# Selective scan on one NeuronCore: two states per VectorE scan where the products with C are on VectorE, over two PSUM banks

## The chip, the cores and the metric

The kernel runs on one core of a Trainium2 chip. The metric is the device time of one execution in microseconds.

## The reference

The whole network is a vision state-space block (layer 0) followed by linear attention and a small quantized feed-forward (layer 1), on 8 images of 96 channels and 64 x 64 pixels. Nearly all of the time goes into the selective scan of layer 0. For each image, for 4 directions k, 192 inner channels d and 16 states n, over the 4096 positions l:

```
delta = softplus(dts + dt_bias)                 # one step size per (k, d, l)
dA    = exp(delta * A)                          # A < 0, one per (k, d, n)
h     = dA * h + (delta * u) * B[k, n, l]       # the recurrence over l
y     = sum over n of h * C[k, n, l]  +  D * u
```

The four directions are rows and columns of 8 x 8 windows, each forward and backward. The four y are added. Layer norms, convolutions, a gate and the two products of layer 1 surround this.

## The kernel before

**Tiles.** A direction of an image is cut into 8 chunks of T = 512 positions. One chunk of one direction is a *unit*: 8 images x 4 directions x 8 chunks = 256 units, worked one after the other. A unit has 192 x 16 sequences. 128 partitions hold 64 channels for two halves of the states, so there are 3 groups of channels (j) and, for each, 8 columns of states, in two groups (g) of G = 4. That makes six *tiles* of four states: `TILES` lists (g, j). A unit runs through 24 *slots*, one for each state of each tile: slot = 4n + m.

**A slot.** Four engines work on a state:

- POOL (`inputs`, L946) makes `hb`, the input (delta u) x B of a whole tile, 128 x 2048, in SBUF.
- ScalarE (`decays`, L1062) makes `da` = exp(delta x A), 128 x 512, in a PSUM bank, for the slot two ahead. `da` has three banks.
- VectorE (L1123) scans: it runs the recurrence with `tensor_tensor_scan`, starting from the column of `carry` that holds the state's last value in the chunk before. Backward directions use reversed views.
- The product with C comes in two ways. For the first `u.banked[n]` states of tile n the scan writes back into the PSUM bank, and VectorE multiplies by C into `hb` (L1125). For the others the scan writes into `hb`, and POOL multiplies later (`outputs`, L952). `BANKED` gives the numbers by tile: 4, 0, 4, 0, 4, 2 in most units, and 4, 0, 4, 0, 4, 1 in the first eight units of each image but the first.

The last value of each state goes to `carry` by a ScalarE copy: one per state of the first kind, out of PSUM (L1126), one per tile for the rest, out of `hb` (L1131). The copy is put on `kept` and issued at the start of the next slot, in front of that slot's decay.

**The sums.** TensorE adds the products over the states into two PSUM banks, tagged y01 and y2 (`sums`, L972), adds the skip part D x u, or the y of a pass before, fetched by `before`, with an identity or diagonal matrix (L981), and ScalarE takes the result out (`gather`, L989 and L992).

**Step sizes.** `step_sizes` is a chain of six steps: a TensorE product into a bank of its own (tag dt, L911), Abs, Exp and Ln on ScalarE (L919, L921, L923), one VectorE step (L925), and the product with u on POOL (L928). Kind "a" is done once per unit (128 channels), kind "b" once per two units (64 channels of each). `spread` then copies delta and delta u to both halves of the partitions by DMA (L940). `fetched_dt`, `fetched_u` and `fetched_pair` load the chain's inputs (L886, L893, L899), `states` loads B and C, repeated over 64 partitions (L880).

**Order.** Each engine's instructions run in the order in which the program issues them. `plan` lists by hand what is issued in each slot after the scan, for this unit, the one before (`last`), the next (`nxt`) and the one after (`third`). After each slot, `advance` lets two side streams go on: the back end of the image before and the front end of the next one. SP issues all DMAs. [...] three for da, one for dt, f0 and f1 for the side streams, y01 and y2 for the sums.

Of the kernel before, what the change touches and what calls it, by code (L numbers as in the profile page):

```python
# [9 lines left out]
F32 = mybir.dt.float32  # L10
# [3 lines left out]
ALU = mybir.AluOpType  # L14
# [16 lines left out]
SPREAD = 5  # L31
HB = 6

BANKED = ((4, 0, 4, 0, 4, 1), (4, 0, 4, 0, 4, 2))

HOLD = 3
LAND = 11
# [6 lines left out]
def kernel(ctx: ExitStack, tc: tile.TileContext, a, out):  # L44
# [13 lines left out]
    dram = ctx.enter_context(tc.tile_pool(name="scratch", bufs=2, space=DRAM))  # L58
    psum = ctx.enter_context(tc.tile_pool(name="psum", bufs=1, space=PSUM))

    BANKS = {"da": 3, "dt": 1, "f0": 1, "f1": 1, "y01": 1, "y2": 1}

    def bank(tag, name):
        return psum.tile([P, T], F32, tag=tag, name=name, bufs=BANKS[tag])
# [9 lines left out]

    eps = const([P, 1], 1e-5, "eps")
    one = const([P, 1], 1.0, "one")
    ones_c = const([C, C], 1.0 / C, "ones_c")

    def centering(n, m, diagonal, name):
# [766 lines left out]
    for b in range(out.shape[0]):  # L846
        s = {"b": b, "done": set(), "live": b + 1 == out.shape[0]}
        images.append(s)
        for pair in (1, 0):
            for back in range(2):  # L850
                for i in range(NC):
                    u = Unit()
                    u.s, u.pair, u.back, u.k = s, pair, back, pair + 2 * back
                    u.c, u.start = (NC - 1 - i if back else i), i == 0
                    u.new, u.i = (pair, back, i) == (1, 0, 0), len(units)
                    u.bc, u.hb, u.delta, u.du = {}, {}, {}, {}
                    u.banked = BANKED[int(b == 0 or u.i % 32 >= NC)]
                    units.append(u)

    TILES = [(g, j) for g in range(2) for j in range(3)]  # L860
# [40 lines left out]
    def step_sizes(us, i):  # L901

        u, which = us[0], "ab"[len(us) - 1]
        if i == 0:
            u.ps = bank("dt", "dt")
            if which == "a":
                todo = [(u.ps, slice(0, P), u)]
            else:
                todo = [(u.ps[64 * h : 64 * h + 64], slice(P, DI), w) for h, w in enumerate(us)]
            for ps, d, w in todo:  # L910
                nc.tensor.matmul(ps, dt_w[32 * w.k : 32 * w.k + R + 1, d], w.dts, start=True, stop=True)  # L911
            u.nat = sp.tile([P, T], F32, tag="nat" + which, name="nat", bufs=1)
            if which == "a":
                u.nata = u.nat
            else:
                for w in us:
                    w.natb = u.nat
        elif i == 1:
            nc.scalar.activation(u.nat, u.ps, AF.Abs)  # L919
        elif i == 2:  # L920
            nc.scalar.activation(u.nat, u.nat, AF.Exp, scale=-1.0)  # L921
        elif i == 3:
            nc.scalar.activation(u.nat, u.nat, AF.Ln, bias=one)  # L923
        elif i == 4:
            nc.vector.scalar_tensor_tensor(u.nat, u.ps, 0.0, u.nat, ALU.max, ALU.add)  # L925
        else:
            x = u.ua if which == "a" else u.ub
            nc.gpsimd.tensor_tensor(x, u.nat, x, ALU.mult)  # L928
# [19 lines left out]
    def outputs(u, n):  # L948

        lo = u.banked[n]  # L950
        hb = u.hb[n][:, lo:, :]
        nc.gpsimd.tensor_tensor(hb, hb, u.bc[1, TILES[n][0]][:, lo:, :], ALU.mult)  # L952

    def before(u):

        src = u.s["u"][1] if u.k == 1 else u.s["y"][u.pair]
        u.plain = []
        for i, rows in enumerate((slice(0, P), slice(P, src.shape[0]))):
            t = sp.tile([P, T], F32, tag=f"u{i}", name=f"u{i}", bufs=1)[: rows.stop - rows.start]
            u.plain.append(into(t, src[rows, bass.ts(u.c, T)]))  # L960

    def sums(u, ns, m):

# [7 lines left out]
        for ps, n, i in todo:  # L971
            nc.tensor.matmul(  # L972
                ps, halves, u.hb[n][:, i, :], start=TILES[n][0] == 0 and m == 0, stop=False, skip_group_check=True
            )
        if ns[-1] == 5 and m == 1:
            first = u.k == 1
            for ps, w, x in (
                (u.p[0], dd_a if first else ident, u.plain[0]),
                (u.p[1][low] if first else u.p[1], dd_b if first else ident, u.plain[1]),
            ):  # L980
                nc.tensor.matmul(ps, w, x, start=False, stop=True, skip_group_check=True)  # L981

    def gather(u, i):

# [12 lines left out]
    def plan(u, last, nxt, third):  # L997

        at = [[] for _ in range(24)]

        def put(slot, f, *args):
            at[slot].append((f, args))

        if last:
            put(0, outputs, last, 5)
            put(0, before, last)
            for m in range(2):
                put(m, sums, last, (3, 4), 2 + m)
            for m in range(2):
                put(5 + m, sums, last, (5,), m)  # L1010
            put(7, states, u, 1, 1)
            put(10, gather, last, 0)
            put(11, gather, last, 1)
        for n in range(6):
            to = (u, n + 2) if n < 4 else (nxt, n - 4)
            if to[0]:
                put(4 * n + 1, inputs, *to)
        if third and u.i % 2:
            put(16, step_sizes, (nxt, third), 5)
        put(8, outputs, u, 1)  # L1020
        put(16, outputs, u, 3)
        for m in range(4):
            put(13 + m, sums, u, (0, 1), m)
            if m < 2:
                put(18 + m, sums, u, (2,), m)
                put(22 + m, sums, u, (3, 4), m)
        if nxt:
            for i, slot in enumerate((0, 2, 4)):
                put(slot, step_sizes, (nxt,), i + 3)
            put(4, spread, nxt, 0, (0, 1))  # L1030
            put(6, spread, nxt, 1, (0, 1))
            put(10, states, nxt, 0, 0)
            put(15, states, nxt, 1, 0)
            put(20, states, nxt, 0, 1)
            if u.i % 2 == 0:
                put(15, spread, nxt, 0, (2,))
                put(16, spread, nxt, 1, (2,))
        if third:
            put(1, fetched_dt, third)
            put(9, fetched_u, third)  # L1040
            for i, slot in enumerate((20, 22, 23)):
                put(slot, step_sizes, (third,), i)
            if u.i % 2:
                for i, slot in enumerate((9, 11, 12, 13, 15)):
                    put(slot, step_sizes, (nxt, third), i)
                put(17, spread, nxt, 0, (2,))
                put(18, spread, nxt, 1, (2,))
            elif u.i + 3 < len(units):
                put(21, fetched_pair, third, units[u.i + 3])
        return at  # L1050

    def at_index(i):
        return units[i] if 0 <= i < len(units) else None

    def decays(q):

        if q >= 24 * len(units):
            return
        u, (n, m) = units[q // 24], divmod(q % 24, G)
        g, j = TILES[n]  # L1060
        da[q] = bank("da", "da")
        nc.scalar.activation(  # L1062
            da[q], u.delta[j], AF.Exp, scale=a_neg[:, u.k, j, g * G + m : g * G + m + 1]
        )

    da, kept, side, carry = {}, [], [], None
    for u in units[:2]:
        fetched_dt(u)
    fetched_u(units[0])
# [6 lines left out]
    for what in range(2):  # L1076
        spread(units[0], what, range(3))
    fetched_u(units[1])
    for i in range(3):
        step_sizes(units[1:2], i)  # L1080
    inputs(units[0], 0)
    inputs(units[0], 1)
    decays(0)
    decays(1)

    def advance(n):

# [4 lines left out]
    for u in units:  # L1092
        last, nxt, third = (at_index(u.i + d) for d in (-1, 1, 2))
        if u.new:
# [7 lines left out]
            else:  # L1102
                final = back_end(b, u.s)
                last_kit = back_kit(None, "f0", True, kit_f)
                side.append(Stream(final[0][0](last_kit, range(1, NC)[::-1])))
        if third and third.new:
            drained(*side[-1:])
            all_issued()
        if u.start:
            carry = sp.tile([P, 24], F32, tag="carry", name="carry")  # L1110
        todo = plan(u, last, nxt, third)
        for slot in range(24):
            n, m = divmod(slot, G)
            g, j = TILES[n]
            q, hb, first_at = 24 * u.i + slot, u.hb[n], 0 if u.back else T - 1
            col = carry[:, 8 * j + g * G + m : 8 * j + g * G + m + 1]
            while kept:
                kept.pop(0)()
            decays(q + 2)
            d = da.pop(q)  # L1120
            banked = m < u.banked[n]
            dd, x = (d[:, ::-1], hb[:, m, ::-1]) if u.back else (d, hb[:, m, :])
            nc.vector.tensor_tensor_scan(dd if banked else x, dd, x, 0.0 if u.start else col, ALU.mult, ALU.add)  # L1123
            if banked:
                nc.vector.tensor_tensor(hb[:, m, :], d, u.bc[1, g][:, m, :], ALU.mult)  # L1125
                kept.append(lambda col=col, d=d, at=first_at: nc.scalar.copy(col, d[:, at : at + 1]))  # L1126
            elif m == G - 1:
                lo = 8 * j + g * G
                kept.append(
                    lambda c=carry[:, lo + u.banked[n] : lo + G].unsqueeze(2), h=hb[:, u.banked[n] :, :], at=first_at:  # L1130
                    nc.scalar.copy(c, h[:, :, at : at + 1])  # L1131
                )
            for f, args in todo[slot]:
                f(*args)
            place[0] = slot
# [2 lines left out]
    for f in kept:  # L1138
        f()
    outputs(u, 5)  # L1140
    before(u)
    for m in range(2):
        sums(u, (3, 4), 2 + m)
    for m in range(2):
        sums(u, (5,), m)
    gather(u, 0)
    gather(u, 1)
    all_issued()
# [76 lines left out]
```

## Time and profile before

| | |
|---|---|
| runs before (3) | 11338.22 / 11342.24 / 11354.75 us, median 11342.24 |
| the profiled execution | 11372.37 us, span of its instructions 11370.7 us |
| the scan phase | from 352 to 11092 us |
| granted TensorE clock | 0.822 |
| DMA engines, mean busy share in the scan phase | 0.85 |

The profile is one execution. Part 1 of the page has each engine's busy time, part 5 the groups of instructions by line with their count, mean duration and the idle time just before them with what ended it. The chain of waits lists which engine and line waited for which, the total in us, how often, and the longest. A line of the timeline has start and duration in us, engine, line, operation, what is written and read.

### The profile page before, as it was taken

How to read it: one execution, taken by the hardware profiler on the slowest of the kernel's cores; microseconds unless marked ns; L12 is line 12 of the kernel's file. 1: busy time of each engine (PE TensorE's matmuls, PEld its weight loads, DVE VectorE, ACT ScalarE, POOL GpSimd, SP SyncE). 2: the span in 40 equal slices, each digit the busy share in tenths (PEclk: the TensorE clock that was granted, in tenths of full speed). 3: DMA queues.
4: the chain of work that ended last, by engine and by line, in shares of the span. 5: the costliest groups of instructions: out<-in, count | busy, mean ns of one | idle time of the engine just before them, and what ended most of it. 6: DMA issues, size and time to landing. Idle time of an engine off the chain costs nothing. (4 is left out here: it accounts for less than half of the span.)

```text
span 11370.7 us, 97041 instructions
## 1 busy us (share of the span) xinstructions
PE 8567.3 (75%) x23270; PEld 2328.5 (20%) x23270; DVE 10367.4 (91%) x10828; ACT 7508.4 (66%) x14939; POOL 10398.7 (91%) x2783
## 2 busy tenths in 40 slices
PE   6577657887778877888678876788768887676677
PEld 2111112222122211222112221222212221111122
DVE  0799999999999999999999999999999999999991
ACT  3566656767666676667766676666766667666674
POOL 0799999999999999999999999999999999999990
PEclk8678778888788877889778887888878888787787
DMA  2788878898888888888888888889888888888872
GB/s 71 171 197 197 201 189 210 209 225 196 203 210 212 219 198 202 210 215 215 195 207 210 216 214 194 210 205 228 202 200 211 212 220 195 198 198 195 201 188 78
DMA packets 1081039, 2253.24 MB, mean 198 GB/s; under 512 B 419609, under 2 KB 420314, under 8 KB 949395
## 3 DMA queue, kind: packets, MB, share of 16 engines
q1 hardware_dynamic: 1080467, 2247.05, 81.3%
q8 instruction: 184, 3.01, 0.1%
q14 instruction: 388, 3.18, 0.1%
HBM read 1507.14 MB, written 336.69 MB: 162 GB/s over the span
## 5 line engine op out<-in xcount | busy, mean ns | idle before, releaser
L946 POOL TENSOR_TENSOR hb<-b,du 128x2048 f32<-128x2048 f32 x1536 | 6939.0, 4535 | 21.3 <-DMA du<-ua 14.3
L1062 ACT ACTIVATE da<-delta,w_a_logs 128x512 f32<-128x512 f32 x6144 | 4216.7, 689 | 696.3 <-DVE hb L1123 575.8
L972 PE MATMUL p<-hb,halves 128*64 128x512 f32 x12288 | 3822.7, 731 | 800.1 <-POOL hb L952 382.1
L1123 DVE TENSOR_TENSOR_SCAN da<-da,carry,hb 128x512 f32<-128x512 f32 x3087 | 3949.0, 1279 | 58.0 <-ACT da L1062 54.3
L952 POOL TENSOR_TENSOR hb<-hb,c 128x2048 f32<-128x2048 f32 (+2 forms) x768 | 2984.9, 3887 | 304.7 <-ACT carry L1131 252.2
L1123 DVE TENSOR_TENSOR_SCAN hb<-da,carry,hb 128x512 f32<-128x512 f32 x2289 | 2781.0, 1264 | 57.7 <-ACT da L1062 56.7
L1125 DVE TENSOR_TENSOR hb<-da,c 128x512 f32<-128x512 f32 x3528 | 2440.5, 692 | 154.0 <-DVE da L1123 0.9
L1126 ACT COPY carry<-da 128x1 f32<-128x1 f32 x3528 | 554.9, 157 | 2351.6 <-DVE hb L1125 2341.1
L972 PEld LDWEIGHTS p<-hb,halves 128*64 128x64 f32 x12288 | 916.2, 161 | 3540.7 <-issue 2129.5
L434 PE MATMUL conv<-f0im,taps 97*128 97x512 f32 (+1 forms) x2088 | 903.5, 664 | 95.9 <-ACT f0pre L490 54.3
L928 POOL TENSOR_TENSOR ua<-nat,ua 128x512 f32<-128x512 f32 x256 | 327.3, 1279 | 257.5 <-DMA b<-xd 257.5
L1123 DVE TENSOR_TENSOR_SCAN da<-da,hb 128x512 f32<-128x512 f32 x441 | 537.7, 1219 | 26.0 <-POOL hb L946 24.6
L925 DVE SCALAR_TENSOR_TENSOR nat<-dt,nat 128x512 f32<-128x512 f32 x384 | 259.5, 676 | 238.9 <-ACT nat L923 238.9
L911 PE MATMUL dt<-dts,dt_w 7*64 7x512 f32 (+1 forms) x1024 | 450.0, 657 | 16.9 <-DVE nat L925 12.4
L981 PE MATMUL p<-u,ident 128*128 128x512 f32 x768 | 438.3, 699 | 3.6 <-DMA u<-y 3.6
L376 PE MATMUL ctr<-f1b,cen_c 96*96 96x512 f32 x460 | 271.9, 697 | 193.4 <-DVE f1b L769 158.8
L434 PEld LDWEIGHTS conv<-f0im,taps 97*128 97x128 f32 (+1 forms) x2088 | 254.6, 174 | 681.6 <-issue 523.5
L1123 DVE TENSOR_TENSOR_SCAN hb<-da,hb 128x512 f32<-128x512 f32 x327 | 377.9, 1204 | 4.9 <-ACT da L1062 4.9
L382 PE MATMUL var<-f1b,ones_c 96*96 96x512 f32 x346 | 207.4, 684 | 153.6 <-ACT f1b L379 145.3
L792 POOL TENSOR_TENSOR f1b<-f1b,f1o 96x512 f32<-96x512 f32 x58 | 67.7, 1167 | 252.0 <-ACT f1o L790 251.9
L1131 ACT COPY carry<-hb 128x4 f32<-128x4 f32 (+2 forms) x768 | 146.8, 191 | 197.4 <-DVE hb L1123 184.8
L655 PE MATMUL cab<-f1m,cab_w 96*96 96x512 f32 x348 | 206.0, 719 | 90.9 <-ACT f1b L664 41.4
(416 smaller groups left out, 7710.5 us busy)
## 6 DMA issues: line engine op xcount, KB each, us to landing
b<-xd SPq DMA_DIRECT2D x1024, 512.0 KB
c<-xd SPq DMA_DIRECT2D x1024, 512.0 KB
delta<-nat SPq DMA_DIRECT2D x1536, 128.0 KB
du<-ua SPq DMA_DIRECT2D x1024, 128.0 KB
y<-yt SPq DMA_DIRECT2D x512, 256.0 KB
u<-y SPq DMA_DIRECT2D x384, 256.0 KB
ua<-u SPq DMA_DIRECT2D x256, 256.0 KB
du<-ub SPq DMA_DIRECT2D x512, 128.0 KB
```

Source lines behind the costliest of these rows:

```text
L376: nc.tensor.matmul(ps, cen_c, src, start=i == 0, stop=i == len(srcs) - 1)
L434: nc.tensor.matmul(ps, taps[:, t, lo : lo + n], im[:, r0 + dy : r0 + dy + 8, dx : dx + HW], start=t == 0, stop=t == 8,)
L911: nc.tensor.matmul(ps, dt_w[32 * w.k : 32 * w.k + R + 1, d], w.dts, start=True, stop=True)
L928: nc.gpsimd.tensor_tensor(x, u.nat, x, ALU.mult)
L946: nc.gpsimd.tensor_tensor(hb, u.bc[0, g], u.du[j].unsqueeze(1).to_broadcast([P, G, T]), ALU.mult)
L952: nc.gpsimd.tensor_tensor(hb, hb, u.bc[1, TILES[n][0]][:, lo:, :], ALU.mult)
L972: nc.tensor.matmul(ps, halves, u.hb[n][:, i, :], start=TILES[n][0] == 0 and m == 0, stop=False, skip_group_check=True)
L981: nc.tensor.matmul(ps, w, x, start=False, stop=True, skip_group_check=True)
L1062: nc.scalar.activation(da[q], u.delta[j], AF.Exp, scale=a_neg[:, u.k, j, g * G + m : g * G + m + 1])
L1123: nc.vector.tensor_tensor_scan(dd if banked else x, dd, x, 0.0 if u.start else col, ALU.mult, ALU.add)
L1125: nc.vector.tensor_tensor(hb[:, m, :], d, u.bc[1, g][:, m, :], ALU.mult)
L1126: kept.append(lambda col=col, d=d, at=first_at: nc.scalar.copy(col, d[:, at : at + 1]))
```

## The change

In units whose product counts allow it, states with products on VectorE are taken in pairs. `da` becomes two tiles of two banks each. A scan of 1024 elements runs over both banks of a pair, and one product of 1024 elements follows. So that the second state of the pair does not go on from the first's last value, the element at the border gets its decay set to zero, and the carry it would have had is put in by ScalarE beforehand: the input at that element becomes input + decay x carry (an Identity activation of one element), and then zero is copied over the decay. In the first unit of a pass there is no carry, and only the zero is written. One ScalarE copy then takes both last values to `carry`. States with products on POOL are scanned singly as before, out of one half of a pair tile.

The counts become 4, 0, 4, 0, 4, 2 in the first eight units of each image but the first, and in the other units 4, 0, 4, 0, 4, 2 and 4, 0, 4, 0, 4, 4 in turn.

With four banks for da the dt bank is gone: the chain of kind "a" writes into the y01 bank and that of kind "b" into y2, between a gather and the next sums. For that, `plan` moves the gathers from slots 10 and 11 to 4 and 8, the first sums from slots 13 to 16 to slots 15 and 16, those of tile 2 one slot later, and the step sizes to slots 6 to 20 of the unit before their use (kind "b" one slot later than now). The addition of the skip part becomes a function of its own (`added`, slots 2 and 6), its fetch is made in the unit itself (slots 18 and 21) and not at slot 0 of the next; `spread` for the first two groups moves from slots 4 and 6 to 2 and 3, `fetched_u` from 9 to 5, `fetched_dt` to slot 14 of the unit before. At the end of an image the front stream is drained one unit earlier.

```diff
-BANKED = ((4, 0, 4, 0, 4, 1), (4, 0, 4, 0, 4, 2))
+BANKED = (((4, 0, 4, 0, 4, 2),), ((4, 0, 4, 0, 4, 2), (4, 0, 4, 0, 4, 4)))
...
-    BANKS = {"da": 3, "dt": 1, "f0": 1, "f1": 1, "y01": 1, "y2": 1}
+    BANKS = {"f0": 1, "f1": 1, "y01": 1, "y2": 1}
...
-                    u.banked = BANKED[int(b == 0 or u.i % 32 >= NC)]
+                    some = BANKED[int(b == 0 or u.i % 32 >= NC)]
+                    u.banked = some[u.i % len(some)]
...
-            u.ps = bank("dt", "dt")
+            u.ps = bank({"a": "y01", "b": "y2"}[which], "dt")
...
         lo = u.banked[n]
+        if lo == G:
+            return
...
+            put(2, added, last, 0)
+            put(4, gather, last, 0)
...
+            put(6, added, last, 1)
+            put(8, gather, last, 1)
             put(7, states, u, 1, 1)
-            put(10, gather, last, 0)
-            put(11, gather, last, 1)
+        if nxt:
+            put(2, spread, nxt, 0, (0, 1))
+            put(3, spread, nxt, 1, (0, 1))
+        if third:
+
+            put(5, fetched_u, third)
+            for i, slot in enumerate((6, 8, 9, 10, 12, 20)):
+                put(slot, step_sizes, (third,), i)
+            if u.i % 2:
+                for i, slot in enumerate((10, 12, 13, 14, 16, 17)):
+                    put(slot, step_sizes, (nxt, third), i)
...
-            put(13 + m, sums, u, (0, 1), m)
+        for m, slot in enumerate((15, 15, 16, 16)):
+            put(slot, sums, u, (0, 1), m)
             if m < 2:
-                put(18 + m, sums, u, (2,), m)
+                put(19 + m, sums, u, (2,), m)
                 put(22 + m, sums, u, (3, 4), m)
+        put(18, before, u, 0)
+        put(21, before, u, 1)
...
+        fourth = at_index(u.i + 3)
+        if fourth:
+            put(14, fetched_dt, fourth)
+            if u.i % 2 == 0:
+                put(21, fetched_pair, third, fourth)
...
-        da[q] = bank("da", "da")
+        if m % 2 == 0:
+            da[q // 2] = psum.tile([P, 2, T], F32, tag="da", name="da", bufs=2)
+        d = da[q // 2]
         nc.scalar.activation(
-            da[q], u.delta[j], AF.Exp, scale=a_neg[:, u.k, j, g * G + m : g * G + m + 1]
+            d[:, m % 2, :], u.delta[j], AF.Exp, scale=a_neg[:, u.k, j, g * G + m : g * G + m + 1]
         )
+        if m % 2 and m < u.banked[n]:
+
+
+            i, at = (0, T - 1) if u.back else (1, 0)
+            edge, col = d[:, i, at : at + 1], column(j, g, m - 1 + i)
+            if not u.start:
+                x = u.hb[n][:, m - 1 + i, at : at + 1]
+                nc.scalar.activation(x, edge, AF.Identity, bias=x, scale=carry[0][:, col : col + 1])
+            nc.scalar.copy(edge, zero)
...
+    def scanned_state(u, slot):
+
+        n, m = divmod(slot, G)
+        g, j = TILES[n]
+        q, hb = 24 * u.i + slot, u.hb[n]
+        end = slice(0, 1) if u.back else slice(T - 1, T)
+        while kept:
+            kept.pop(0)()
+        decays(q + 2)
+        banked = m < u.banked[n]
+        if banked and m % 2:
+            return
+        pair = da[q // 2] if m % 2 == 0 else da.pop(q // 2)
+        if banked:
+            col = column(j, g, m + u.back)
+            d, x = (t.rearrange("p m l -> p (m l)") for t in (pair, hb[:, m : m + 2, :]))
+        else:
+            col = column(j, g, m)
+            d, x = pair[:, m % 2, :], hb[:, m, :]
+        if u.back:
+            d, x = d[:, ::-1], x[:, ::-1]
+        init = 0.0 if u.start else carry[0][:, col : col + 1]
+        nc.vector.tensor_tensor_scan(d if banked else x, d, x, init, ALU.mult, ALU.add)
+        if banked:
+            nc.vector.tensor_tensor(hb[:, m : m + 2, :], pair, u.bc[1, g][:, m : m + 2, :], ALU.mult)
+            del da[q // 2]
+            ends, lo, hi = pair, m, m + 2
+        elif m == G - 1:
+            ends, lo, hi = hb[:, u.banked[n] :, :], u.banked[n], G
+        else:
+            return
+        to = carry[0][:, column(j, g, lo) : column(j, g, hi)].unsqueeze(2)
+        kept.append(lambda: nc.scalar.copy(to, ends[:, :, end]))
...
-        if third and third.new:
+        if u.i + 3 < len(units) and units[u.i + 3].new:
             drained(*side[-1:])
             all_issued()
```

More of the change, by code (lines that the diff above doesn't have):

```diff
@@ L76 @@
     one = const([P, 1], 1.0, "one")
+    zero = const([P, 1], 0.0, "zero")
     ones_c = const([C, C], 1.0 / C, "ones_c")
@@ L855 @@
                     u.new, u.i = (pair, back, i) == (1, 0, 0), len(units)
-                    u.bc, u.hb, u.delta, u.du = {}, {}, {}, {}
-                    u.banked = BANKED[int(b == 0 or u.i % 32 >= NC)]
+                    u.bc, u.hb, u.delta, u.du, u.plain = {}, {}, {}, {}, {}
+                    some = BANKED[int(b == 0 or u.i % 32 >= NC)]
+                    u.banked = some[u.i % len(some)]
                     units.append(u)
@@ L950, in outputs, with before, added @@
         lo = u.banked[n]
+        if lo == G:
+            return
         hb = u.hb[n][:, lo:, :]
         nc.gpsimd.tensor_tensor(hb, hb, u.bc[1, TILES[n][0]][:, lo:, :], ALU.mult)
-    def before(u):
+    def before(u, i):
         src = u.s["u"][1] if u.k == 1 else u.s["y"][u.pair]
[L957 to L960, printed above, removed]
+        rows = (slice(0, P), slice(P, src.shape[0]))[i]
+        t = sp.tile([P, T], F32, tag=f"u{i}", name=f"u{i}", bufs=1)[: rows.stop - rows.start]
+        u.plain[i] = into(t, src[rows, bass.ts(u.c, T)])
+    def added(u, i):
+        ps, first = u.p[i], u.k == 1
+        w = ((dd_a, dd_b)[i]) if first else ident
+        nc.tensor.matmul(
+            ps[0:64] if first and i else ps, w, u.plain[i], start=False, stop=True, skip_group_check=True
+        )
     def sums(u, ns, m):
@@ L974, in sums @@
             )
[L975 to L981, printed above, removed]
     def gather(u, i):
@@ L1005, in plan @@
             put(0, outputs, last, 5)
-            put(0, before, last)
             for m in range(2):
                 put(m, sums, last, (3, 4), 2 + m)
+            put(2, added, last, 0)
+            put(4, gather, last, 0)
             for m in range(2):
                 put(5 + m, sums, last, (5,), m)
+            put(6, added, last, 1)
+            put(8, gather, last, 1)
             put(7, states, u, 1, 1)
-            put(10, gather, last, 0)
-            put(11, gather, last, 1)
+        if nxt:
[8 more added lines that the diff above has]
+                    put(slot, step_sizes, (nxt, third), i)
         for n in range(6):
@@ L1017, in plan @@
                 put(4 * n + 1, inputs, *to)
-        if third and u.i % 2:
-            put(16, step_sizes, (nxt, third), 5)
         put(8, outputs, u, 1)
         put(16, outputs, u, 3)
-        for m in range(4):
-            put(13 + m, sums, u, (0, 1), m)
+        for m, slot in enumerate((15, 15, 16, 16)):
+            put(slot, sums, u, (0, 1), m)
             if m < 2:
-                put(18 + m, sums, u, (2,), m)
+                put(19 + m, sums, u, (2,), m)
                 put(22 + m, sums, u, (3, 4), m)
+        put(18, before, u, 0)
+        put(21, before, u, 1)
         if nxt:
[L1028 to L1031, printed above, removed]
             put(10, states, nxt, 0, 0)
@@ L1037, in plan @@
                 put(16, spread, nxt, 1, (2,))
[L1038 to L1045, printed above, removed]
-                put(17, spread, nxt, 0, (2,))
-                put(18, spread, nxt, 1, (2,))
-            elif u.i + 3 < len(units):
-                put(21, fetched_pair, third, units[u.i + 3])
+            else:
+                put(17, spread, nxt, 0, (2,))
+                put(19, spread, nxt, 1, (2,))
+        fourth = at_index(u.i + 3)
[3 more added lines that the diff above has]
+                put(21, fetched_pair, third, fourth)
         return at
@@ L1053, in at_index, with column @@
         return units[i] if 0 <= i < len(units) else None
+    def column(j, g, m):
+        return 8 * j + g * G + m
     def decays(q):
@@ L1060, in decays @@
         g, j = TILES[n]
-        da[q] = bank("da", "da")
+        if m % 2 == 0:
+            da[q // 2] = psum.tile([P, 2, T], F32, tag="da", name="da", bufs=2)
+        d = da[q // 2]
         nc.scalar.activation(
-            da[q], u.delta[j], AF.Exp, scale=a_neg[:, u.k, j, g * G + m : g * G + m + 1]
+            d[:, m % 2, :], u.delta[j], AF.Exp, scale=a_neg[:, u.k, j, g * G + m : g * G + m + 1]
         )
-    da, kept, side, carry = {}, [], [], None
+        if m % 2 and m < u.banked[n]:
[5 more added lines that the diff above has]
+            nc.scalar.copy(edge, zero)
+    da, kept, side, carry = {}, [], [], [None]
     for u in units[:2]:
@@ L1078 @@
     fetched_u(units[1])
-    for i in range(3):
-        step_sizes(units[1:2], i)
     inputs(units[0], 0)
@@ L1084 @@
     decays(1)
+    for i in range(6):
+        step_sizes(units[1:2], i)
+    fetched_dt(units[2])
+    def scanned_state(u, slot):
[26 more added lines that the diff above has]
+            ends, lo, hi = hb[:, u.banked[n] :, :], u.banked[n], G
+        else:
+            return
+        to = carry[0][:, column(j, g, lo) : column(j, g, hi)].unsqueeze(2)
+        kept.append(lambda: nc.scalar.copy(to, ends[:, :, end]))
     def advance(n):
@@ L1109 @@
         if u.start:
-            carry = sp.tile([P, 24], F32, tag="carry", name="carry")
+            carry[0] = sp.tile([P, 24], F32, tag="carry", name="carry")
         todo = plan(u, last, nxt, third)
         for slot in range(24):
[L1113 to L1132, printed above, removed]
+            scanned_state(u, slot)
             for f, args in todo[slot]:
@@ L1140 @@
     outputs(u, 5)
-    before(u)
     for m in range(2):
@@ L1145 @@
         sums(u, (5,), m)
+    for i in range(2):
+        added(u, i)
     gather(u, 0)
```

## The prediction

> **What bounds the kernel now.** I read the page's part 1 first, then the busy times over the scan phase (first to last scan, 352 to 11092 us), then the groups, then the chain of waits, then the timeline.
>
> ```profile
> PE 8567.3 (75%) x23270; PEld 2328.5 (20%) x23270; DVE 10367.4 (91%) x10828; ACT 7508.4 (66%) x14939; POOL 10398.7 (91%) x2783
> ```
>
> ```profile
> 352.00:11092.00 10740.00, 8145.56 (x22246) 2185.72 (x22245) 10313.25 (x10697) 7281.15 (x14607) 10371.12 (x2747) 0.82 0.85 205
> ```
>
> The second line has PE, PEld, DVE, ACT, POOL in that order. In the 10740 us of scans VectorE is busy 10313 (96%) and POOL 10371 (97%): the two share the bound, and nothing before or after that phase changes here. The groups say what VectorE does and how little it waits:
>
> ```profile
> L1123 DVE TENSOR_TENSOR_SCAN da<-da,carry,hb 128x512 f32<-128x512 f32 x3087 | 3949.0, 1279 | 58.0 <-ACT da L1062 54.3
> L1123 DVE TENSOR_TENSOR_SCAN hb<-da,carry,hb 128x512 f32<-128x512 f32 x2289 | 2781.0, 1264 | 57.7 <-ACT da L1062 56.7
> L1125 DVE TENSOR_TENSOR hb<-da,c 128x512 f32<-128x512 f32 x3528 | 2440.5, 692 | 154.0 <-DVE da L1123 0.9
> ```
>
> VectorE waits about 115 us in all for decays, because ScalarE runs two states ahead: in the trace the median decay ends 2.3 us before its scan. That lead is what the change spends. The decisive row is in the chain of waits:
>
> ```profile
> ACT carry L1126 <- DVE hb L1125: 2341.1, 2311, 4.1
> ```
>
> The carry copy reads what the scan (L1123) wrote, yet it waits for the product (L1125). The timeline, VectorE first and then ScalarE in the same three microseconds:
>
> ```profile
> 5518.47 1.28 DVE L1123 TENSOR_TENSOR_SCAN da<-da,carry,hb 128x512 f32<-128x512 f32 x1
> 5519.79 0.69 DVE L1125 TENSOR_TENSOR hb<-da,c 128x512 f32<-128x512 f32 x1
> 5520.40 1.28 DVE L1123 TENSOR_TENSOR_SCAN da<-da,carry,hb 128x512 f32<-128x512 f32 x1
> ```
>
> ```profile
> 5520.51 0.16 ACT L1126 COPY carry<-da 128x1 f32<-128x1 f32 x1 [1.04 <-DVE hb L1125]
> 5520.71 0.69 ACT L1062 ACTIVATE da<-delta,w_a_logs 128x512 f32<-128x512 f32 x1
> ```
>
> The scan ends at 5519.75, the product at 5520.48, the copy starts at 5520.51, and the decay queued behind it follows. Over all 3528 pairs in the trace no copy starts earlier than 33 ns after the product's end; those that waited started 33 to 35 ns after it.
>
> [...] The changed copy and product also read the same two banks. [...]
>
> **The change, part by part.**
>
> *Counts.* States with products on VectorE: before 56 units x 13 + 200 x 14 = 3528. After: 56 x 14 + 100 x 14 + 100 x 16 = 3784, in 1892 pairs. The other states fall from 2616 to 2360.
>
> *VectorE's own work.* I use start-to-start times in the trace: a single scan 1.175 us; scan to product 1.316; product to next scan 0.608; so 1.924 per state with a product. A product of 1024 elements: L227, a tensor_tensor of 1728 elements, took 1957 ns against 692 for 512, a slope of 1.04 ns, so +0.533. The scan has no second size in the trace. If its fixed part is that of the product (0.075) plus what the carry operand adds (1279 - 1219 = 0.06), 1.040 us remain for 512 elements; I take +1.06. A pair then takes 1.316 + 1.06 + 0.608 + 0.533 = 3.52 us, against 2 x 1.924 = 3.85. Saved: 1892 x 0.33 = **-624**. Bounds: -0.22 per pair (scan saves nothing) to -0.40: -420 to -760. The 256 states that come over cost 256 x (1.924 - 1.175) = **+192**.
>
> *POOL* loses those 256 products at 2984.9 / 2616 = 1.14 us: -292. That would matter only if POOL remained the bound.
>
> *The new wait.* Decays are issued two states ahead. With pairs, slot m of a pair issues the next pair's first decay, and slot m+1 first issues this pair's carry copy, then the next pair's second decay, then (new) the edge: an Identity of one element with two pointer operands that adds decay x carry to the input, and a copy of zero into the decay. ScalarE takes them in that order, and the next scan needs all of them. So where a pair follows a pair, from the product's end: 0.033 to the copy, 0.19 copy to decay (median spacing), 0.689 decay, 0.03 for the dependent next (L369 to L370: 675 ns apart, 642 long), 0.33 the fix (0.157 for a one-element copy, plus two operands at about 0.09), 0.03, 0.157 the zero, 0.033 to the scan: 1.49 us. Without a wait the scan would have started 0.084 before the product's end. The stall is **1.58 us**; in the first unit of each pass (1 in 8), which has no fix, 1.22. Mean 1.535. Bounds 1.33 (the two small ones overlap) to 1.75 (each takes 0.1 more).
>
> How often: the order of tiles is 4, 0, 4, 0, 4, then 2 or 4 states. Pair follows pair inside tiles 0, 2, 4 and from tile 4 to 5: 4 times. With 4 in tile 5 also inside it and on into the next unit: 6. So 156 x 4 + 100 x 6 = 1224 times x 1.535 = **+1879** (1628 to 2140). Queued behind the waiting copy on ScalarE are that decay, the edge and whatever side work follows; POOL and PE are not held by it. Where a single follows a pair, its decay came in the even slot: no stall.
>
> *What fills the stall.* Other VectorE work in those slots (643 side instructions in the trace; by its slots about 35% fall there, plus the 128 step-size steps moved to slot 16): 353 x 0.6 = **-212** (0 to -300).
>
> *Pair after singles*, 668 times: ScalarE has two single scans, 2.35 us, for two decays and the edge, 1.93, so 0.42 us are left for side work. By slot that averages 0.2 to 0.6 us and comes in lumps: I put 0.15 us each, **+100** (0 to 250).
>
> *Waits that go*: the 115 us for decays are counted anew above: **-120**.
>
> *Moved and free.* Step sizes run in slots 6 to 20 of the unit before instead of 20 to 4; counts are equal. POOL's step product (1.28 us) now stands between two input products, which in the trace end a median 5.8 us before their scan. SP's fetch of ua comes two slots after the transfer that reads it instead of three; SP waits 74.5 us for that now, and the next loads behind it have 14 slots (25 us) to their use. The skip inputs (u) are fetched some five slots earlier, dt thirteen. The step sizes take the sums' banks, so their matmul waits for the gathers (slots 4 and 8, before 10 and 11) and the next sums for the step. In PE's order the last sums and the skip need about 11 us between slots 22 and 4; six slots give 10.6 us today, 12 in the slower kernel. I take **0**, bounds 0 and +250. The fetch of the image after is drained one unit earlier: 0.
>
> *Sum*: -624 + 192 + 1879 - 212 + 100 - 120 = **+1215**. The profiled execution took 11372.37 (span 11370.7), 30 above the median of 11342.24; I add the difference to the median: 12557, rounded to **12,560 us**.
>
> **Rivals.**
>
> *The copy leaves when the scan ends* (would be **faster**). If copy and product were not kept apart, the same 1.49 us would start at the scan's end, and 1.26 us of it lie under the product. The stall would be 0.32 x 1224 = +390, with some 100 us of it filled: -624 + 192 + 390 - 100 + 100 - 120 = -162, **11,180**. The change gains whenever the stall is below (624 - 192 - 100 + 120) / 1224 = 0.37 us. Against it: every one of 3528 copies. For it: only that the pair's copy is a new form.
>
> *Shared banks as well*: ScalarE's gather at slots 4 and 8 meets a PE that is not done, and stands in front of the decays. PE already waits 403.7 + 317.2 us for gathers (L992). At 1 to 2 us in each of 256 units: +250 to +500 on the forecast, **12,900**.
>
> *The scan is no cheaper in pairs*: +204 on the forecast, 12,760; inside my range.
>
> **How the numbers follow.** The forecast with its bounds has 0.80 (12,200 to 12,850), shared banks 0.13, the early copy 0.05, the rest 0.02. The range 12,200 to 12,950 leaves out the early copy and the far end of shared banks. 0.2% (23 us) is about what a measurement of this kernel can tell from no change; faster 0.05, same 0.02, slower 0.93.
>
> **What would show it.** Right: VectorE's busy time falls to about 9.9 ms while the span grows; its idle before the pair scans reaches about 1.9 ms, released by ScalarE; the copy of two carries starts 33 ns after the 1225 ns product; POOL falls to about 10.1 ms and idles. Wrong: copies that start inside a product, pairs 3.5 us apart throughout, a scan of 1024 elements near 2.5 us, or the new idle time ended by PE or POOL.

## The result, and the profile after

The changed kernel takes **13347.54 us** (median of 4 runs, 13346.72 to 13349.42), against 11348.49 before on the same chips: 1.1758 times, 95% interval 1.1745 to 1.1772. It is slower, as forecast and by the kind of wait forecast, but by 1999 us and not by the 1215 forecast; 13,348 lies 400 us above the range.

Parts 1 and 5 of the page of the changed kernel (span 13346.2 us, profiled execution 13347.91 us):

```profile
PE 8989.0 (67%) x23270; PEld 2417.2 (18%) x23270; DVE 10181.3 (76%) x7301; ACT 7904.5 (59%) x16763; POOL 10110.0 (76%) x2683
...
L1130 DVE TENSOR_TENSOR_SCAN da<-da,carry,hb 128x1024 f32<-128x1024 f32 x1668 | 3924.1, 2353 | 1666.4 <-ACT da L1085 1457.6
...
L1130 DVE TENSOR_TENSOR_SCAN hb<-da,carry,hb 128x512 f32<-128x512 f32 x2040 | 2496.6, 1268 | 462.9 <-ACT da L1074 448.6
L1140 ACT COPY carry<-da 128x2 f32<-128x2 f32 x1892 | 303.2, 160 | 4094.3 <-DVE hb L1132 4093.7
L1132 DVE TENSOR_TENSOR hb<-da,c 128x1024 f32<-128x1024 f32 x1892 | 2317.2, 1225 | 103.1 <-DVE da L1130 1.8
```

VectorE and POOL have less to do than before (10181 and 10110 us) and both idle a quarter of the time. The idle time of VectorE stands before two groups: the scans of pairs, released by L1085, the zero copied into the decay at the border, and the single scans, released by L1074, a decay. The chain of waits has the cause and both effects:

```profile
ACT carry L1140 <- DVE hb L1132: 4093.7, 1751, 7.1
...
DVE da L1130 <- ACT da L1085: 1610.0, 1176, 5.3
...
DVE hb L1130 <- ACT da L1074: 532.4, 657, 3.1
```

ScalarE waits 4094 us for products in order to copy carries, and VectorE waits for what stands behind those copies. One pair after another on the timeline, VectorE and then ScalarE:

```profile
6008.69 1.23 DVE L1132 TENSOR_TENSOR hb<-da,c 128x1024 f32<-128x1024 f32 x1
6011.37 2.36 DVE L1130 TENSOR_TENSOR_SCAN da<-da,carry,hb 128x1024 f32<-128x1024 f32 x1 [1.45 <-ACT da L1085]
6013.77 1.23 DVE L1132 TENSOR_TENSOR hb<-da,c 128x1024 f32<-128x1024 f32 x1
6014.91 0.25 DVE L736 TENSOR_TENSOR gram<-gram 97x97 f32<-97x97 f32 x1
6015.94 4.81 DVE L1130 TENSOR_TENSOR_SCAN hb<-da,carry,hb 128x512 f32<-128x512 f32 x4 [0.78 <-ACT da L1074]
```

```profile
6010.01 0.16 ACT L1140 COPY carry<-da 128x2 f32<-128x2 f32 x1 [2.86 <-DVE hb L1132]
6010.06 0.70 ACT L1074 ACTIVATE da<-delta,w_a_logs 128x512 f32<-128x512 f32 x1
6010.79 0.35 ACT L1084 ACTIVATE hb<-da,hb,carry 128x1 f32<-128x1 f32 x1
6011.18 0.16 ACT L1085 COPY da<-zero 128x1 f32<-128x1 f32 x1
6011.27 0.69 ACT L1074 ACTIVATE da<-delta,w_a_logs 128x512 f32<-128x512 f32 x1
6015.08 0.16 ACT L1140 COPY carry<-da 128x2 f32<-128x2 f32 x1 [3.12 <-DVE hb L1132]
6015.14 1.31 ACT L1074 ACTIVATE da<-delta,w_a_logs 128x512 f32<-128x512 f32 x2
```

The first product ends at 6009.92; copy, decay, fix and zero follow, and the next scan starts at 6011.37. After the second product, at 6015.00, a single follows. Its own decay had run from 6011.27 to 6011.96. Yet the scan starts at 6015.94, when the *other* decay of that two-bank tile, issued behind the copy, is done.

Counted over the scan phase, VectorE's idle time by what comes after what ("pair" is a scan with its product on VectorE; before the change that is one state):

| idle us before | before | changed |
|---|---|---|
| pair after pair | 111 (2760 times) | 1717 (1223) |
| single after pair | 25 (768) | 563 (668) |
| pair after single | 23 (767) | 182 (668) |
| single after single | 114 | 46 |
| product after its scan | 154 | 103 |
| sum | 427 | 2610 |

The scan phase grew from 10740 to 12736 us: 2183 us more idle, 187 less busy.

### The profile page after: what moved, and what is told of

Read it like the earlier page. It is cut to its first block, busy times and chain, and to the rows that moved or that the text cites. A ratio compares the mean times of both kernels' runs of the same rounds, so it can differ in the third digit from the quotient of the medians.

```text
span 13346.2 us, 97562 instructions
## 1 busy us (share of the span) xinstructions
PE 8989.0 (67%) x23270; PEld 2417.2 (18%) x23270; DVE 10181.3 (76%) x7301; ACT 7904.5 (59%) x16763; POOL 10110.0 (76%) x2683
## 5 line engine op out<-in xcount | busy, mean ns | idle before, releaser
L948 POOL TENSOR_TENSOR hb<-b,du 128x2048 f32<-128x2048 f32 x1536 | 6917.5, 4519 | 149.7 <-issue 77.2
L1130 DVE TENSOR_TENSOR_SCAN da<-da,carry,hb 128x1024 f32<-128x1024 f32 x1668 | 3924.1, 2353 | 1666.4 <-ACT da L1085 1457.6
L956 POOL TENSOR_TENSOR hb<-hb,c 128x2048 f32<-128x2048 f32 (+1 forms) x668 | 2681.0, 4013 | 2480.1 <-issue 1435.3
L1074 ACT ACTIVATE da<-delta,w_a_logs 128x512 f32<-128x512 f32 x6144 | 4192.7, 689 | 424.5 <-DVE hb L1130 389.5
L1130 DVE TENSOR_TENSOR_SCAN hb<-da,carry,hb 128x512 f32<-128x512 f32 x2040 | 2496.6, 1268 | 462.9 <-ACT da L1074 448.6
L1140 ACT COPY carry<-da 128x2 f32<-128x2 f32 x1892 | 303.2, 160 | 4094.3 <-DVE hb L1132 4093.7
L1132 DVE TENSOR_TENSOR hb<-da,c 128x1024 f32<-128x1024 f32 x1892 | 2317.2, 1225 | 103.1 <-DVE da L1130 1.8
L913 PE MATMUL dt<-dts,dt_w 7*128 7x512 f32 (+1 forms) x1024 | 527.4, 769 | 521.7 <-ACT yt L995 298.9
L1084 ACT ACTIVATE hb<-da,hb,carry 128x1 f32<-128x1 f32 x1668 | 586.4, 352 | 111.7 <-ACT da L1074 3.0
L1130 DVE TENSOR_TENSOR_SCAN da<-da,hb 128x1024 f32<-128x1024 f32 x224 | 513.4, 2292 | 155.9 <-ACT da L1085 152.4
L1085 ACT COPY da<-zero 128x1 f32<-128x1 f32 x1892 | 308.0, 163 | 59.6
L779 PE MATMUL ff<-f1x,q_w 96*128 96x512 fp8e5 x174 | 84.9, 488 | 358.6 <-ACT f1h L781 199.2
```

The costliest lines, as they stand in the source:

```text
L948: nc.gpsimd.tensor_tensor(hb, u.bc[0, g], u.du[j].unsqueeze(1).to_broadcast([P, G, T]), ALU.mult)
L1074: nc.scalar.activation(d[:, m % 2, :], u.delta[j], AF.Exp, scale=a_neg[:, u.k, j, g * G + m : g * G + m + 1])
L1084: nc.scalar.activation(x, edge, AF.Identity, bias=x, scale=carry[0][:, col : col + 1])
L1130: nc.vector.tensor_tensor_scan(d if banked else x, d, x, init, ALU.mult, ALU.add)
L1132: nc.vector.tensor_tensor(hb[:, m : m + 2, :], pair, u.bc[1, g][:, m : m + 2, :], ALU.mult)
```

## The experiments

The kernels below are the changed kernel with one edit, unless said otherwise. Kernel medians are set against the kernel before on the same chip.

**1. The copy behind the decay.** Three kernels exchange the order in the odd slot of a pair: everywhere, only where a single follows, only where a pair follows. The comment in the edit marks the second and third; `pair_next` says that the next slot's state is taken in a pair.

```diff
-        while kept:
-            kept.pop(0)()
-        decays(q + 2)
         banked = m < u.banked[n]
+        early = banked and m % 2 == 1     # and not pair_next / and pair_next
+        if early:
+            decays(q + 2)
+        while kept:
+            kept.pop(0)()
+        if not early:
+            decays(q + 2)
```

Everywhere: 

> In the odd slot of a pair ScalarE gets the next decay and its edge first, and the carry copy after them; nothing else is changed. Theory (the copy waits for the pair's product and holds the decay behind it): both waits go, 1717 us of idle time before pairs that follow pairs and 563 us before singles that follow pairs. The side work that lay in them (322 us) comes back onto VectorE's path: 13347 - 2280 + 322 - 160 (overlap of product and next scan regained) = about 11,230, between 11,050 and 11,400. Rival (ScalarE is held by gathers and by the step sizes that share the sums' banks, not by the copy): at least 12,800.

Measured 11489.54 us (1.0121 of before, 1.0104 to 1.0138). Idle before a pair after a pair 383 us, before a single after a pair 73 us.

Only before singles: 

> The same exchange only where a single scan follows the pair; where a pair follows, the copy stays in front. Theory A (the first single scan waits for both decays of its pair of banks, and the second of these stands behind the copy): the 563 us before singles go, and their 102 us of side work and 56 us of overlap count back: about 12,830. Theory B (the first single waits for its own decay, late for other reasons): no change, 13,250 to 13,350.

Measured 12918 us (one run, before 11352). The wait before singles went from 563 to 56 us, and the other stayed (1750). This is what theory A said.

Only before pairs: 

> The same exchange only where a pair follows the pair. Theory (copy in front of the decay): the 1717 us before pairs go, 220 us of side work come back, 103 us of overlap are regained: about 11,750, with the waits before singles still near 560 us. Rival (shared banks hold ScalarE): above 13,000.

Measured 11898 us (one run). Before pairs 370 us, before singles 547. The two waits are separate and add: -429 and -1450 against -1858 together. So the order of copy and decay carries 1858 of the 1999 us, and no theory in which PE or the shared banks hold ScalarE is left for these.

With the exchange everywhere, the theory's size was too hopeful by 260 us: with the order exchanged the kernel is still slower than before, and 861 us of idle time remain, twice the 427 of before. One place on its timeline, ScalarE and then VectorE:

```profile
6018.12 0.69 ACT L1074 ACTIVATE da<-delta,w_a_logs 128x512 f32<-128x512 f32 x1
6018.83 1.28 ACT L398 ACT_TABLE_LOAD   x1
6020.12 1.49 ACT L443 ACTIVATE f0pre<-f0pre 128x1536 f32<-128x1536 f32 x1
6021.62 1.28 ACT L398 ACT_TABLE_LOAD   x1
6022.92 0.69 ACT L1074 ACTIVATE da<-delta,w_a_logs 128x512 f32<-128x512 f32 x1
```

```profile
6021.15 1.22 DVE L1136 TENSOR_TENSOR hb<-da,c 128x1024 f32<-128x1024 f32 x1
6024.23 2.36 DVE L1134 TENSOR_TENSOR_SCAN da<-da,carry,hb 128x1024 f32<-128x1024 f32 x1 [1.85 <-ACT da L1085]
```

A lump of 4.05 us (two table loads and a silu) lies between the two decays of a pair; the scan that needs both waits 1.85 us. How much of the 861 us such lumps carry was not counted.

**2. The edge left out.** `decays` loses the fix and the zero, so this kernel does not compute the same thing and only measures what the edge costs.

> Leaves out the edge: the input at the border is not corrected and the decay there not set to zero, so the second state goes on from the first. The order is that of the changed kernel. Theory (a chain of copy, decay, fix, zero from the product's end to the next scan): the chain of 1.46 us loses the fix (0.38) and the zero (0.16) and their spacing, 0.58 in all, 1223 times, some 700 us less: about 12,600, and the wait of a pair after a pair falls to that of a single after a pair, 0.85 to 0.9 us. If the edge's own cost were the main thing: 11,700 or less.

Measured 12584 us (one run): 763 less than the changed kernel. The wait of a pair after a pair has a median of 0.88 us (1.46 with the edge), that of a single after a pair still 0.89. So 1.46 us is 0.88 of copy and decay and 0.58 of edge. Of the idle time that goes, 631 us stood before pairs after pairs and 113 before pairs after singles.

**3. By tile or by bank.** The copy stays in front, and the second single's decay is issued after the first single's scan:

```diff
-        decays(q + 2)
         banked = m < u.banked[n]
+        n1, m1 = divmod((slot + 1) % 24, G)
+        late = banked and m % 2 == 1 and m1 >= u.banked[n1]
+        if not late:
+            decays(q + 2)
...
         nc.vector.tensor_tensor_scan(d if banked else x, d, x, init, ALU.mult, ALU.add)
+        n0, m0 = divmod(slot - 1, G)
+        if slot and not banked and m0 < u.banked[n0]:
+            decays(q + 1)
```

> The changed kernel with the carry copy in front of the next decay, as it is, but where singles follow a pair the second single's decay is issued only after the first single's scan. Theory (waits are kept by tile: a scan that reads one bank of a two-bank tile waits for all that was issued into the tile before it, and a decay into the other bank waits for that scan): the 563 us before the first single go, and about as much appears before the second one (0.033 + 0.689 + 0.033 after the first scan's end, 668 times, 450 to 520 us): 13,200 to 13,350. Rival (waits are kept by bank, and the first single was late for its own decay): the 563 us stay where they are; or, if by bank and the second decay was the cause, they go and nothing takes their place: about 12,900.

Measured 13326 us (one run, before 11356). Before the first single 42 us are left, and single after single rose from 46 to 491: the wait moved, as it must if both the scan's wait for decays and the decay's wait for the scan go by the two-bank tile. One place, VectorE and then ScalarE:

```profile
6018.11 1.27 DVE L1133 TENSOR_TENSOR_SCAN hb<-da,carry,hb 128x512 f32<-128x512 f32 x1
6020.15 1.28 DVE L1133 TENSOR_TENSOR_SCAN hb<-da,carry,hb 128x512 f32<-128x512 f32 x1 [0.18 <-ACT da L1074]
```

```profile
6019.42 0.69 ACT L1074 ACTIVATE da<-delta,w_a_logs 128x512 f32<-128x512 f32 x1 [0.31 <-DVE hb L1133]
```

The decay for the second bank starts 0.04 us after the scan of the first bank ends. Over all 668 places its start comes a median 34 ns after that end, and never less than 33.

**4. The new order of work alone.** Scans of one state over three banks and the old counts, with the step sizes in the sums' banks and all work at its new slots.

> The new order of work alone: step sizes in the sums' banks, gathers, sums, spreads and fetches at their new slots, but scans of one state over three banks and the old counts (13 or 14), as before. Theory (the shared banks and the new slots cost little): 11,330 to 11,450. Rival (they hold ScalarE between PE and the decays): 11,600 to 11,850.

Measured 11281.75 us, **0.9944** of before (0.9928 to 0.9961): faster, which neither side expected. Idle time fell from 427 to 368 us, and the fall is in single after single (114 to 45); VectorE's own work was unchanged (10314 and 10306 us).

**5. The copy on VectorE, and ScalarE's lumps elsewhere.** VectorE copies a pair's carries after its product:

```diff
+        if banked:
+            nc.vector.tensor_copy(to, ends[:, :, end])
+        else:
+            kept.append(lambda: nc.scalar.copy(to, ends[:, :, end]))
-        kept.append(lambda: nc.scalar.copy(to, ends[:, :, end]))
```

> The changed kernel, with the pair's two carries copied by VectorE after its product; ScalarE has no copy that waits for a product. Theory (that one wait in ScalarE's order is what costs): the waits after pairs go as with the exchange, VectorE gets 1892 small copies at 0.06 to 0.16 us (110 to 300 us), and ScalarE, which still waited 2065 us for products in the exchanged order, comes to its side work sooner, so less is left of that kernel's 861 us of idle time: 11,300 to 11,550. Rival (the idle time left is set by POOL or PE): the copies come on top, 11,600 to 11,800.

Measured 11403.74 us, 1.0055 of before (1.0040 to 1.0070), inside the theory's range: 102 us more of VectorE work than with the exchanged order, 182 us less idle.

With the exchanged order (first kernel of part 1), the side work moved:

```diff
-    CALM = (0, 1, 8, 9, 16, 17)
+    CALM = (1, 9, 17)
-            put(8, gather, last, 1)
+            put(9, gather, last, 1)
-            for i, slot in enumerate((6, 8, 9, 10, 12, 20)):
+            for i, slot in enumerate((6, 9, 11, 12, 14, 20)):
```

> The exchanged order, and ScalarE's heavy side work moved out of even slots of pairs: the slots in which the table loads with silu and gelu may run become 1, 9, 17 (from 0, 1, 8, 9, 16, 17), the second gather goes from slot 8 to 9, and steps 1 to 4 of the step sizes from slots 8, 9, 10, 12 to 9, 11, 12, 14. Theory (what is left is ScalarE late with the second decay of a pair, most of it before the scan at slot 10, 202 us): 150 to 300 us less than 11,490, 11,200 to 11,350. Rival (POOL sets it): within 50 us of 11,490.

Measured 11541.28 us (1.0175), slower than without the move: a miss. The wait before slot 10 fell from 202 to 79 us, but those before slots 12 and 14 rose from 29 and 13 to 124 and 160. In the odd slots the copy stands in front of this side work, so it can hold it until the product is done, and the decays after it too (in the exchanged order ScalarE's copies waited 2065 us for products). That is only part of the rise: without the copy on ScalarE (next kernel, against the one before with VectorE's copy) the same move also raised the waits before slots 12 and 14, from 31 to 161 us together.

Both together, VectorE's copy and the moved side work:

> VectorE's carry copy and the moved side work together. If the two reliefs add: 11,100 to 11,350; if they relieve the same wait: no better than the better one of the two alone.

Measured 11315.32 us, 0.9971 (0.9961 to 0.9981). Without a copy that waits, the same move gained 88 us, and 521 us of idle time are left.

The same without the edge:

> VectorE's carry copy and the moved side work (11,315), with the edge left out (no correction of the input at the border, no zero in the decay). Theory (with the long wait gone, what is left of the loss is ScalarE late by the 0.55 us of the edge in front of pairs): the idle time before pairs (89 and 114 us) mostly goes, 11,120 to 11,230. Rival (POOL or the shared slots set it): 11,280 or more.

Measured 11179.34 us, 0.9840 (0.9821 to 0.9860). Idle before pairs fell from 204 to 122 us, in all from 521 to 422. The edge costs about 140 us here (136 by the times, 149 by the ratios to the kernel before), where it cost 763 behind the copy. Without the edge the second state of a pair goes on from the first, so this is a measure of the edge and not a kernel to use.

With the edge again, and fewer products on VectorE:

> VectorE's carry copy and the moved side work (11,315), with 4, 0, 4, 0, 4, 2 in all units: 200 products less on VectorE and as many more on POOL. VectorE loses 200 x 0.75 = 150 us, POOL gains 200 x 1.14 = 228 us and is busy 10,340. Theory (the two engines share the bound, and their work is balanced at 16 and 14 in turn): 11,350 to 11,500. If VectorE alone set the time: 11,170.

Measured 11293.29 us, 0.9948 (0.9933 to 0.9962): no worse than with more products on VectorE. VectorE's phase lost 81 us of work and gained 41 of idle time. Neither number held. POOL's part is open. The first view below has the scan phase, with PE, PEld, DVE, ACT and POOL in that order; the second has waits for the inputs that POOL makes (L948), of a pair's scan on VectorE and of the fix on ScalarE (L1084):

```profile
353.00:11027.00 10674.00, 8026.23 (x22237) 2157.11 (x22237) 10111.31 (x8961) 7580.02 (x14438) 10302.96 (x2747) 0.82 0.84 206
```

```profile
DVE da L1130 <- POOL hb L948: 64.2, 67, 2.5
ACT hb L1084 <- POOL hb L948: 84.9, 108, 1.7
```

POOL is busy 10303 of 10674 us (97%) and VectorE 10111 (95%). With the larger counts VectorE's wait was 32 us and that of ScalarE's fix 4. So POOL does hold some of the pairs now; how much of the time it sets was not tested.

Last, that kernel with steps 1 to 4 of kind a in slots 9, 10, 11, 12:

> The kernel with VectorE's carry copy, moved side work and 4, 0, 4, 0, 4, 2 (11,293), with steps 1 to 4 of kind a in slots 9, 10, 11, 12 and no longer 9, 11, 12, 14, where they met kind b's in slots 12 and 14. Theory (what is left of the idle time is ScalarE's lumps): the waits before slots 12 and 14 (161 us in the kernel with the larger counts) shrink by half, 11,200 to 11,270, which is below the new order alone (11,282). Rival (they only move to another slot): 11,280 to 11,340.

Measured 11302.22 us, 0.9960 (0.9946 to 0.9973), where the rival had it. Single after single fell from 108 to 54 us of idle time, pair after single rose from 180 to 248. POOL's inputs ended 90 us of the waits of pair scans here, so whether the waits only moved from slot to slot, or POOL held them, is not settled. Of the kernels that compute the same thing, the new order without pairs is at 0.9944, and the best with pairs, at 0.9948, is level with it.

**Where the gain of pairs went.** Against the new order alone, pairs with the two reliefs (0.9971) have 114 us less of VectorE work (10192 against 10306) and 153 us more idle time. From start to start a pair saves 0.314 us, 594 us in all; the 256 added products spend 192 of it, and the carry copies on VectorE 127 (0.067 us each). The remaining 275, and 39 more, are lost in waits and in the overlap that goes with them: the scan phase is 10713 us against 10674. The edge is about 140 of that; what sets the rest was not taken apart.

## Why the prediction was right or wrong

- **The copy waits for the product**: right. Over 1892 pairs no copy started earlier than 32 ns after its product's end; the median is 88 ns, where 33 was put. What keeps the two apart, no run shows.
- **Counts**: right. 1668 + 224 = 1892 pair scans, 2040 + 320 = 2360 singles, 1223 times pair after pair against 1224.
- **VectorE's own work**: right. Scan to product 2.392 us against the 2.376 summed, product to next 1.142 against 1.141. The scan over two banks took 2353 ns against 1279 for one state before, 1.074 us more (1.06 put); what the second bank itself costs, no run shows. The busy time of about 9.9 ms, given as a sign of being right, was missed all the same: it was 10.18. A scan that waits no longer overlaps the product before it (a median 0.084 us before the change), which adds 103 us of busy time where a pair follows and 56 where a single does. And 51 us of the saving lie in the gaps between scan and product, which are idle time and not work.
- **The chain of 1.49 us**: right, 1.46 in the median, with some luck: its parts differed and made up for each other. The copy started 0.088 after the product (0.033 put), the decay started 0.057 after the copy (0.19 put), the fix 0.731 after the decay (0.72; 0.764 over all 1668 pairs that have one), the zero 0.383 after the fix (0.36). The 0.09 put for each of the fix's two operands was an estimate from two rows of before, Exp at 617 ns without an operand of one column (L921) and Ln at 710 with one (L923). The fix took 352 ns (L1084) and the copy of zero 163 (L1085): by the same estimate 0.09 each.
- **Where a single follows a pair, no stall**: this is the step that failed. Measured 563 us of idle time, and with it 668 x 0.084 = 56 us of lost overlap between product and next scan. The decay of the first single was indeed early. What was missed is that its scan waits for both decays issued into the two-bank tile, and the second stood behind the copy: in none of the 668 places does the scan start earlier than 32 ns after the end of that second decay, nor earlier than 0.83 us after the end of its own. The two partial exchanges and the late decay show it.
- **What fills the stall, -212**: too hopeful. Stalls without side work on VectorE last 1.506 us on average, those with one such instruction 1.763 from product to scan, with the same median of 1.456: a minority of long ones makes the difference. That ScalarE has a lump of work there is likely but was not counted. In the prediction's own terms the idle time before a pair after a pair was 1879 - 212 - 103 of overlap = 1564; it was 1717.
- **Pair after singles, +100**: 159 us more than before.
- **Waits that go, -120**: 204 by the table (111, 25 and 68), as the new waits above are counted whole. Of these only single after single, 68, went for good; the others were replaced by longer ones.
- **Shared banks and slots at nothing, bounds 0 and +250**: the sign was wrong. Alone they gain 0.56%. I had put the lower bound at 0 with no reason that excludes a gain; the rival that built on them, 12,900, was the nearest to the time, still 448 us short, and for the wrong cause.
- **The early copy** (11,180) did not happen.

The difference to the forecast is 1999 - 1215 = 784 us. The failed step and its overlap are 619 of it, the fill 153, pairs after singles 59 and VectorE's own work some 30; the waits that go take 84 off. That is 777 in all.

## What to carry to other kernels

When a buffer becomes two banks wide, ask for each reader and writer what it now waits for: a wait kept by tile joins things that were apart. Here a scan of one bank waited for the decay in the other, 563 us before the 668 single scans that follow a pair, and the half that was ready helped none of them. In front of every instruction that waits on another engine, look at what is queued behind it on its own; here the order of two lines in the program was worth 1858 of 13348 us. And a saving on the bounding engine has to be held against the lead of the engine that feeds it: decays that are issued two slots ahead have a lead of one pair.

## What the runs showed that I had not expected

The new order of work by itself, with a bank less for the step sizes, made the kernel 0.56% faster; which of its moves does it was not tested. And a scan of one bank waited for a decay that was being written into the other, 668 times.
